# A GNN layer on one core: the set of blocks with a third quad join goes from each eighth to each fourth, from block 30 to 102

## The chip, the cores and the metric

One core of one Trainium2 chip. The time is the device time of one execution in microseconds (us). Engines are named as the profile names them: PE (matrix products; PEld its weight loads), DVE and ACT (vector and scalar engine), POOL (which issues the indirect DMAs here), SP (which issues plain DMAs).

## The reference

```python
x = -0.0005121 + 1.001 * jax.random.normal(..., (6250, 64), jnp.float32)
src = jnp.concatenate([_s, _d, _loop]); dst = jnp.concatenate([_d, _s, _loop])
_o = jnp.argsort(dst, stable=True)              # 206250 edges, ordered by dst
row, col = src, dst
msg = jnp.concatenate([x[col], edge_attr], axis=1)      # 64 + 64 columns
h = relu(msg @ W1a.T + b1a)                              # 128 columns
h = h @ W1b.T + b1b
sums = segment_sum(h, row, 6250); counts = segment_sum(ones, row, 6250)
agg = sums / maximum(counts, 1.0)[:, None]
z = relu(concatenate([x, agg], axis=1) @ W2a.T + b2a)
z = z @ W2b.T + b2b
out = layernorm(x + concatenate([z, x], axis=1) @ Wr.T + br)
```

Edges come ordered by dst, and the sum is over src, in no order. So each edge's hidden row (128 columns) has to be brought to its src.

## The kernel before

**Blocks and tiles.** The edges are padded to 124 blocks of 13 tiles of 128 edges. `fast_path` runs one loop over k = 0 to 123; loop k computes the hidden rows of block k on PE (`hidden`, line 1385) and ACT evicts them with relu into the buffer `orow` (line 1389). `orow` has four places (`ROWS = 4`): block k uses the place of block k-4. Line 1376, in `low_bits`, is ACT's first write into it in loop k, so it waits until the scatters of block k-4 have read the place.

**Scatter and sum.** A slot in DRAM is worked out for each edge, bin by bin of src (`bins_of`, `counts_of`, `slots`: lines 1059 to 1117 and 1174 to 1221, on DVE and PE). POOL then writes the rows to their slots by indirect DMA, one instruction for one tile of 128 rows (`ones_`, line 1436). Later SP reads full tiles of slots back (`read`, into `rt`), DVE makes a one-hot matrix from the node number that each row carries (`nodes_of`, line 1550), PE multiplies it with the rows (line 1570, "sums"), and the result is added to the bin's total (line 1641). Without joins there would be 124 x 13 scatters of line 1436.

**Joins.** From block 4 to 109 some tiles are joined: three tiles that go together are sorted by PE into quads, rows of four slots, and one scatter of quads (`fours`, line 1408) takes the place of three scatters of line 1436. `joined(k)` is the number of joins in block k:

```python
JOIN_FROM, JOIN_TO = 4, 110
THRICE = (*range(9, 27, 2), *range(34, 99, 8))
def joined(k):
    if not JOIN_FROM <= k < JOIN_TO:
        return 0
    return 3 if k in THRICE else 2
```

`direct(k)` = 13 - 3 x `joined(k)` tiles stay single. A block without joins has 13 scatters, one with two joins 2 + 7 = 9, one with three 3 + 4 = 7. A join costs: compare matrices `marks` (line 1253 on DVE, 1258 and 1259 on ACT), `side` and `rest` columns (lines 1267 to 1274), six products of 512 columns (line 1288) evicted to `rj` (line 1292), eight products that give the rows in quad order one loop later (line 1300, evicted at 1303), and quad ranks (lines 1117 to 1152, 1164 to 1185). Where the join count changes from one block to the next, `starts_at` (lines 924 and 927) refills a small constant on DVE.

**Order of the work.** The order on PE, ACT, DVE and SP is that of the program text in the loop body: in loop k `marks(k, 0)` and counts of block k+1; the first hidden tiles; `join_rows(k-1)`; the first half of a sum; ranks of block k+1; the last hidden tiles; `join(k, i)`; `join_places(k+1)`; the rest of the sum; the scatters of block k-2. On POOL a scheduler interleaves the last scatters of a block with the first of the next. A "pace" (from line 1416) makes the last single scatters of block k wait for a step of PE in loop k+1: with three joins those of columns 10, 11 and 12, with two those of 6, 8, 10 and 12.

**When sums are made.** A planner decides ahead which tiles are read and summed in which loop. Tiles become full by bounds that depend on how many tiles went to single slots and how many to quads, so the stages' due blocks depend on `joined`. Then it hands out groups by a rate:

```python
RATES = {0: 55, 2: 18, 3: 10}
credit += min(RATES[joined(k)], max(tiles_in(queue) - credit, 0) / (until - k))
while queue and credit > 0:
    groups_at[k].append(queue.pop(0))
    credit -= tiles_in(groups_at[k][-1:])
credit = min(credit, 0)
```

What is left, and what only the last blocks fill, is summed behind loop 123 (the sums of a loop show as line 1570, two instructions a tile). Then come the node layers, group by group of bins.

Of the kernel before, what the change touches and what calls it, by code (L numbers as in the profile page):

```python
# [469 lines left out]
LEAD = 2  # L470
JOIN, QUAD, MARKS = 3, 4, 3
JOIN_FROM, JOIN_TO = 4, 110
THRICE = (*range(9, 27, 2), *range(34, 99, 8))
JOINS = 3 if THRICE else 2
PACED = range(PRE, 123)
SIDES, ENATS, CHUNK = 2, 2, 2
# [12 lines left out]
def fast_path(  # L489
# [64 lines left out]
# [5 lines that stand above are left out]
# [1574 lines left out]
```

## Time and profile before

| | |
|---|---|
| median of 3 runs | 1561.95 us (1561.57 to 1563.52) |
| the profiled execution | 1562.71 us, its span 1560.9 us |
| busy PE / PEld | 1435.2 / 1273.7 us (92% / 82%) |
| busy DVE / ACT | 1369.4 / 1120.6 us (88% / 72%) |
| busy POOL | 1134.2 us (73%) |
| scatters of single tiles / of quads | 922 / 230 |

A row of a group reads: line, engine, operation, tile written <- tiles read, count | busy us, mean ns of one | idle time of the engine just before them, and what ended most of it. A row in order of time reads: start us, length us, engine, line, operation, tiles, count, and in brackets the idle time before it and what ended it. The loops of the program are found on PE by the first instruction of line 1113 in each, loop k being the one that works on block k's hidden rows and block k+1's counts.

### The profile page before, as it was taken

The page shows a single profiled execution, that of the slowest core. Times are in us where ns is not written, and L with a number is a line of the kernel's source. Part 1 is how long each engine was busy: PE and PEld are TensorE (multiplying, and loading weights), DVE is VectorE, ACT ScalarE, POOL GpSimd, SP SyncE. Part 2 cuts the span into 40 slices and gives each one's busy share as a digit, 9 for nine tenths or more (in the row PEclk, how much of TensorE's full clock was granted, in tenths as well). Part 3 has the DMA queues.
Part 4 walks back from the last instruction along what each step waited for, and adds up shares of the span by engine and source line. Part 5 has one row for each costly group of instructions (what it writes and reads, how often), then busy time and mean ns, then how long its engine had stood idle before and what let it go on. Part 6 is the DMA issues. An engine that isn't in the chain of part 4 may idle for free.

```text
span 1560.9 us, 33538 instructions
## 1 busy us (share of the span) xinstructions
PE 1435.2 (92%) x10958; PEld 1273.7 (82%) x10958; DVE 1369.4 (88%) x3031; ACT 1120.6 (72%) x2336; POOL 1134.2 (73%) x1215
## 2 busy tenths in 40 slices
PE   6688898879999899899998999999999999999896
PEld 5567777758888788788887888898888899999785
DVE  7589998979999899889998999999999888876786
ACT  3279999979888788787888878887877743432036
POOL 5777777777777777777777777777777777777711
PEclk9699999989999999999999999999999999999998
DMA  8878888868887888787787777676787899998873
GB/s 208 235 233 270 266 268 263 259 223 264 264 259 231 250 260 261 206 247 236 217 251 216 223 220 250 206 246 215 218 260 241 255 340 352 325 351 265 260 231 92
DMA packets 248713, 387.83 MB, mean 248 GB/s; under 512 B 43285, under 2 KB 180311, under 8 KB 248527
## 3 DMA queue, kind: packets, MB, share of 16 engines
q1 hardware_dynamic: 167661, 220.81, 50.4%
q0 software_dynamic: 47904, 122.68, 21.8%
q10 hardware_dynamic: 32962, 42.08, 8.1%
q8 instruction: 90, 1.47, 0.4%
q14 instruction: 96, 0.79, 0.2%
HBM read 214.09 MB, written 171.32 MB: 247 GB/s over the span
## 4 chain that ended last, share of the span: by engine, by line
PE 64%; DMA 13%; DVE 8%; ACT 7%; issue 4%; POOL 2%; SPq 0%; ACTq 0%; DVEq 0%; POOLq 0%
PE h_ps L1570 24%; PE h_ps L1288 13%; PE h_ps L1385 10%; PE h_ps L1300 8%; DMA rows<-orow,rowidx 8%; POOL rows L1436 2%; DMA rt<-rows 2%; DMA rows<-orow,qidx 1%; DVE marks L1253 1%; ACT marks L1258 1%; DVE oh L1550 1%; PE cnt_ps L1113 1%; ACT orow L1303 1%; PE cnt_ps L1114 1%; ACT orow L1389 1%
## 5 line engine op out<-in xcount | busy, mean ns | idle before, releaser
L1436 POOL DMA_INDIRECT rows<-orow,rowidx x922 | 898.7, 975 | 292.1 <-issue 143.0
L1570 PE MATMUL h_ps<-rt,oh 128*128 128x129 f32 x3952 | 487.3, 277 | 35.6 <-DVE oh L1550 9.9
L1570 PEld LDWEIGHTS h_ps<-rt,oh 128*128 128x128 f32 x3952 | 469.7, 193 | 49.6 <-issue 12.8
L1550 DVE TENSOR_TENSOR oh<-ramp,rt 128x768 f32<-128x768 bf16 (+4 forms) x391 | 308.2, 825 | 37.4 <-DMA rt<-rows 36.5
L1253 DVE TENSOR_TENSOR marks<-quad_ramp,ramp 128x1024 fp32r<-128x1024 f32 x230 | 276.6, 1209 | 0.0
L1408 POOL DMA_INDIRECT rows<-orow,qidx x230 | 224.0, 974 | 71.0 <-issue 25.9
L1385 PE MATMUL h_ps<-mv,rhs 124*128 124x128 f32 x1844 | 265.6, 289 | 4.4 <-ACT orow L1389 4.4
L1389 ACT ACTIVATE orow<-h_ps 128x512 f32<-128x512 f32 (+1 forms) x266 | 143.5, 539 | 173.5 <-PE h_ps L1385 163.8
L1288 PE MATMUL h_ps<-marks,side 128*128 128x512 f32 x690 | 261.7, 408 | 0.6 <-ACT mv L1354 0.6
L1300 PE MATMUL h_ps<-mv,rj 128*128 128x130 f32 x1840 | 236.7, 281 | 11.0 <-ACT orow L1389 7.4
L1385 PEld LDWEIGHTS h_ps<-mv,rhs 124*128 124x128 f32 x1844 | 233.2, 198 | 6.0 <-ACT orow L1389 4.6
L1288 PE MATMUL h_ps<-marks,rest 128*64 128x512 f32 x690 | 235.3, 395 | 0.0
L1300 PEld LDWEIGHTS h_ps<-mv,rj 128*128 128x128 f32 x1840 | 220.7, 193 | 16.9 <-ACT orow L1389 10.1
L1292 ACT COPY rj<-h_ps 128x512 f32<-128x512 f32 x230 | 131.5, 588 | 92.9 <-PE h_ps L1288 92.4
L1288 PEld LDWEIGHTS h_ps<-marks,side 128*128 128x128 f32 x690 | 131.0, 190 | 50.9 <-issue 2.1
L1259 ACT ACTIVATE marks<-marks,ones 128x512 fp32r<-128x512 f32 x230 | 166.1, 722 | 7.5
L1258 ACT ACTIVATE marks<-quad_ramp,z_act 128x512 fp32r<-128x512 f32 x230 | 166.0, 722 | 0.3 <-DVE z_act L1164 0.3
L1303 ACT ACTIVATE orow<-h_ps 128x260 f32<-128x260 f32 x460 | 151.4, 388 | 8.7 <-PE h_ps L1300 4.3
L1071 DVE TENSOR_TENSOR_SCAN had<-ramp,bins 128x400 bf16<-128x400 bf16 (+2 forms) x124 | 128.5, 1036 | 19.8 <-ACT bins L1092 6.4
L1338 ACT ACTIVATE rhs<-rhs,from_win 60x896 f32<-60x896 bf16 (+2 forms) x116 | 123.8, 1067 | 2.9
L1340 ACT ACTIVATE rhs<-rhs,ones 60x896 f32<-60x896 f32 (+2 forms) x116 | 123.5, 1065 | 2.9
L1288 PEld LDWEIGHTS h_ps<-marks,rest 128*64 128x64 f32 x690 | 93.7, 136 | 38.1 <-issue 0.6
(195 smaller groups left out, 1603.4 us busy)
## 6 DMA issues: line engine op xcount, KB each, us to landing
rt<-rows SPq DMA_DIRECT2D x194, 390.0 KB
rt<-rows SPq DMA_DIRECT2D x97, 325.0 KB
rows<-padrow ACTq DMA_DIRECT2D x24, 1040.0 KB
rhs<-in_edgeT SPq DMA_DIRECT2D x88, 224.0 KB
enat<-in_edgeJ SPq DMA_DIRECT2D x88, 192.0 KB
rows<-orow,rowidx POOLq DMA_INDIRECT x922
rt<-rows SPq DMA_DIRECT2D x40, 260.0 KB
rt<-rows SPq DMA_DIRECT2D x48, 195.0 KB
```

What stands on the lines that cost most here:

```text
L1253: nc.vector.tensor_tensor(m[:, :n, :], all_q[:, None, :].to_broadcast([P, n, QUAD * P]), z[:, :n, None].to_broadcast([P, n, QUAD * P]), op ...
L1258: nc.scalar.activation(m[:, t, :], all_q, AF.Square, bias=z_acts[k][:, i * JOIN + t : i * JOIN + t + 1], scale=-1.0)
L1259: nc.scalar.activation(m[:, t, :], m[:, t, :], AF.Relu, bias=ones[:, :1], scale=-1.0)
L1288: done[k, f"turn{i}"] = nc.tensor.matmul(ps[: w.shape[1], :], w, m[:, t, :], start=t + p == 0, stop=last and p == 1).ins.name
L1300: done[k, f"join{i}"] = nc.tensor.matmul(ps[:, j, :], rj[:, (g0 + j) * P : (g0 + j + 1) * P], m, start=True, stop=True).ins.name
L1303: nc.scalar.activation(mrow[:, g0 : g0 + 2, :], ps, AF.Relu)
L1385: done[k, c] = nc.tensor.matmul(ps[:, j, :], rhs[:WIDE, of * P : (of + 1) * P], m[:WIDE, :H], start=True, stop=True).ins.name
L1389: nc.scalar.activation(orow_of(k, k0, n)[:, :, :H], ps[:, :n, :], AF.Relu)
L1408: s = nc.gpsimd.indirect_dma_start(out=qep.rows.rearrange("(q r) f -> q (r f)", r=QUAD), out_offset=bass.IndirectOffsetOnAxis(ap=qidx[:, q ...
L1436: s = nc.gpsimd.indirect_dma_start(out=ep_.rows, out_offset=bass.IndirectOffsetOnAxis(ap=rowidx[:, k % RING * BLK + j : k % RING * BLK + j ...
L1550: nc.vector.tensor_tensor(res[:, at_tile : at_tile + nb * n, :], ramp[:, None, :].to_broadcast([P, nb * n, P]), node[:, :, None].to_broadc ...
L1570: m = nc.tensor.matmul(of_bin(b), oh[:, at, :], rows, start=i == 0, stop=i == len(of) - 1)
```

## The change

`THRICE` holds ten more blocks: 30, 38, 46, 54, 62, 70, 78, 86, 94 and 102; 34, 42 and so on to 98 stay, and 9 to 25 too.

```diff
-THRICE = (*range(9, 27, 2), *range(34, 99, 8))
+THRICE = (*range(9, 27, 2), *range(30, 103, 4))
```

In each of the ten, three tiles that had single scatters form a third join. All else follows from `joined(k)`: NJOIN goes from 230 to 240, the scatters of line 1436 from 922 to 892, those of line 1408 from 230 to 240. The edge loads of such a block change shape (64 x 896 to 64 x 512 and 128 x 384 to 128 x 576), not number. `starts_at` is called 20 times more. The planner's input changes with it: stages that were due at blocks 54, 78 and 102 are due at 55, 81 and 107, those of quads at 47, 68, 81 and 94 instead of 49, 70, 84 and 98, and tiles of sums move between loops. In loops 31 to 109 there are 1026 tiles before and 962 after, in 110 to 120 564 and 568, in loop 121 40 and 60, and 40 more behind loop 121. By tiles in a loop, the loops 31 to 109 are: before, 5 with none, 55 with 12, six with 18, two with 20, eight with 24, three others; after, 5 with none, 63 with 12, two with 18, six with 24, three others.

On POOL around block 30 (its rows are read from orow_142; orow_141 is block 29's, orow_143 block 31's; qidx marks a scatter of quads). Before:

```order
L1408 DMA rows_64<-orow_141,qidx 84320x520 x2
L1436 DMA rows_64<-orow_141,rowidx 337280x130
L1436 DMA rows_64<-orow_142,rowidx 337280x130 x2
L1436 DMA rows_64<-orow_141,rowidx 337280x130
L1436 DMA rows_64<-orow_142,rowidx 337280x130
L1436 DMA rows_64<-orow_143,rowidx 337280x130 x2
L1408 DMA rows_64<-orow_142,qidx 84320x520 x2
L1436 DMA rows_64<-orow_142,rowidx 337280x130 x2
```

The same place after:

```order
L1408 DMA rows_64<-orow_141,qidx 85600x520 x2
L1436 DMA rows_64<-orow_141,rowidx 342400x130 x3
L1436 DMA rows_64<-orow_142,rowidx 342400x130 x2
L1436 DMA rows_64<-orow_143,rowidx 342400x130 x2
L1408 DMA rows_64<-orow_142,qidx 85600x520 x3
L1436 DMA rows_64<-orow_142,rowidx 342400x130 x2
L1436 DMA rows_64<-orow_143,rowidx 342400x130 x2
```

Block 30 has seven single scatters and two of quads before, four and three after; its neighbours keep theirs, in a slightly different interleaving.

On PE at the end of loop 30 (marks_155 to 157 are the three compare matrices in rotation, side_158 and rest_160 the columns of block 30), one piece of the difference:

```order
 L1288 MATMUL h_ps<-marks_157,rest_160 64x512 x2
 L1288 MATMUL h_ps<-marks_157,side_158 128x512
+L1288 MATMUL h_ps<-marks_155,side_158 128x512
+L1288 MATMUL h_ps<-marks_155,rest_160 64x512
+L1288 MATMUL h_ps<-marks_155,side_158 128x512
+L1288 MATMUL h_ps<-marks_155,rest_160 64x512 x2
+L1288 MATMUL h_ps<-marks_155,side_158 128x512
```

Six products of 512 columns are added, the third join of block 30; the other nine new blocks get the same.

On PE behind the last hidden tiles (rhs_151 is block 123's, rt and oh a read tile and its one-hot matrix), where only sums are left before the first node group (line 1976):

```order
 L1570 MATMUL h_ps<-rt,oh 128x129 x10
 L1385 MATMUL h_ps<-mv,rhs_151 128x128 x3
-L1570 MATMUL h_ps<-rt,oh 128x129 x241
+L1570 MATMUL h_ps<-rt,oh 128x129 x281
 L1976 MATMUL h_ps<-ident,agg 128x128 x3
 L1570 MATMUL h_ps<-rt,oh 128x129 x3
```

Forty tiles of sums moved from the loops to this place.

## The prediction

> **What bounds the kernel now.** I read the page first, then POOL's own rows in order of time, then the start of each loop on PE, then the waits, and last the end of the program. The page's head and the two groups of scatters:
>
> ```profile
> span 1560.9 us, 33538 instructions
> ...
> PE 1435.2 (92%) x10958; PEld 1273.7 (82%) x10958; DVE 1369.4 (88%) x3031; ACT 1120.6 (72%) x2336; POOL 1134.2 (73%) x1215
> ...
> L1436 POOL DMA_INDIRECT rows<-orow,rowidx x922 | 898.7, 975 | 292.1 <-issue 143.0
> ...
> L1408 POOL DMA_INDIRECT rows<-orow,qidx x230 | 224.0, 974 | 71.0 <-issue 25.9
> ```
>
> By busy share PE leads and POOL looks a quarter idle. But POOL's 1152 scatters have idle time of 292.1 + 71.0 = 363.1 us in front of them, 0.32 each, and its rows show that this is no waiting. Two neighbours, and three rows far from them (start, length, idle before):
>
> ```profile
> 406.68 0.97 POOL L1436 DMA_INDIRECT rows<-orow,rowidx  x1 [0.30 <-PE cnt_ps L1117]
> ...
> 1034.45 0.96 POOL L1436 DMA_INDIRECT rows<-orow,rowidx  x1 [0.30 <-issue]
> 1035.72 0.97 POOL L1436 DMA_INDIRECT rows<-orow,rowidx  x1 [0.30 <-ACT rj L1292]
> ...
> 1456.42 0.96 POOL L1436 DMA_INDIRECT rows<-orow,rowidx  x1 [0.30 <-issue]
> ...
> 1489.46 0.97 POOL L1436 DMA_INDIRECT rows<-orow,rowidx  x1 [0.30 <-issue]
> ```
>
> The gap is 0.30 whatever is named as its releaser, and 1035.72 - 1034.45 = 1.27: one scatter each 1.27 us. The stage from 676.6 to 1259.3 confirms it (columns: length, then busy time and count for PE, PE's loads, DVE, ACT, POOL; then clock, DMA share, GB/s):
>
> ```profile
> 676.60:1259.30 582.70, 563.88 (x4381) 501.39 (x4382) 548.77 (x1198) 475.64 (x935) 443.68 (x457) 1.00 0.77 236
> ```
>
> 457 x 1.27 = 580 of 582.7 us: POOL is issuing without a pause. PE (563.88, 97%) and DVE (548.77, 94%) are nearly as full. Three engines are within a few per cent of each other, so a change that takes from one and gives to two must be summed for each.
>
> How PE is held by POOL: line 1376 writes into the buffer of rows that the scatters of block k-4 have read. ACT waits there, its next eviction is late, and PE stands. The totals of the waits from 342 to 1458 us (us, times, longest), ACT's and PE's:
>
> ```profile
> ACT orow L1376 <- DMA rows<-orow,rowidx: 22.9, 14, 3.2
> ...
> PE h_ps L1570 <- ACT orow L1389: 8.8, 5, 3.6
> PE h_ps L1570 <- ACT orow L1303: 7.3, 3, 4.2
> ...
> PE h_ps L1300 <- ACT orow L1389: 2.6, 3, 1.3
> ```
>
> A single case is loop 46, from 511.44 to 527.64; PE's rows, and ACT's row in it:
>
> ```profile
> 492.31 0.33 PE L1113 MATMUL cnt_ps<-had,less_ones 128*128 128x400 bf16 x1
> 503.36 0.33 PE L1113 MATMUL cnt_ps<-had,less_ones 128*128 128x400 bf16 x1
> 511.44 0.33 PE L1113 MATMUL cnt_ps<-had,less_ones 128*128 128x400 bf16 x1 [0.45 <-DVE ways L1174]
> 518.47 2.95 PE L1570 MATMUL h_ps<-rt,oh 128*128 128x129 f32 x12 [3.64 <-ACT orow L1389]
> 527.64 0.33 PE L1113 MATMUL cnt_ps<-had,less_ones 128*128 128x400 bf16 x1
> ```
>
> ```profile
> 517.72 0.20 ACT L1376 CAST orow<-lo 128x7 f32<-128x7 bf16 x1 [2.95 <-DMA rows<-orow,rowidx]
> ```
>
> Loop 46 took 527.64 - 511.44 = 16.20 us, where loop 44 with the same work took 503.36 - 492.31 = 11.05: a wait of 2.95 on ACT cost 5.15. So 22.9 is a floor of what POOL costs PE this way.
>
> The end of the sums:
>
> ```profile
> 1423.66 9.10 PE L1570 MATMUL h_ps<-rt,oh 128*128 128x129 f32 x80
> ...
> 1437.73 19.67 PE L1570 MATMUL h_ps<-rt,oh 128*128 128x129 f32 x146
> 1464.13 12.55 PE L1570 MATMUL h_ps<-rt,oh 128*128 128x129 f32 x98 [6.73 <-DVE oh L1550]
> ```
>
> PE has summed all it may by 1457.40, then waits 6.73 us for the first rows that need POOL's block 121 (POOL was at 1457.7 then). From 1464.13 on the rest is sums and the node layers, untouched by the change.
>
> **The change part by part.** Sums are made against the profiled execution: 1562.71 us, span 1560.9, so 0.76 above the median of 1561.95.
>
> *POOL.* Ten blocks lose three L1436 scatters each and gain one L1408: 30 - 10 = 20 fewer, 20 x 1.27 = 25.4 us. The order shows no scatter added elsewhere. Rows of block 121 would so be ready at about 1464.13 - 25.4 = 1438.7, if POOL still never waits.
>
> *PE and DVE, the joins.* Around the triple block 90 of before, the loops begin on PE and on DVE at:
>
> ```profile
> 994.98 0.27 PE L1113 MATMUL cnt_ps<-had,less_ones 128*128 128x250 bf16 x1
> 1005.23 0.33 PE L1113 MATMUL cnt_ps<-had,less_ones 128*128 128x400 bf16 x1
> 1016.32 0.33 PE L1113 MATMUL cnt_ps<-had,less_ones 128*128 128x400 bf16 x1
> 1027.36 0.33 PE L1113 MATMUL cnt_ps<-had,less_ones 128*128 128x400 bf16 x1
> 1037.53 0.33 PE L1113 MATMUL cnt_ps<-had,less_ones 128*128 128x400 bf16 x1
> 1050.66 0.33 PE L1113 MATMUL cnt_ps<-had,less_ones 128*128 128x400 bf16 x1
> ```
>
> ```profile
> 995.29 1.21 DVE L1253 TENSOR_TENSOR marks<-quad_ramp,ramp 128x1024 fp32r<-128x1024 f32 x1
> ...
> 1007.03 1.21 DVE L1253 TENSOR_TENSOR marks<-quad_ramp,ramp 128x1024 fp32r<-128x1024 f32 x1
> ...
> 1018.21 1.21 DVE L1253 TENSOR_TENSOR marks<-quad_ramp,ramp 128x1024 fp32r<-128x1024 f32 x1
> ...
> 1028.26 1.21 DVE L1253 TENSOR_TENSOR marks<-quad_ramp,ramp 128x1024 fp32r<-128x1024 f32 x1
> ...
> 1038.31 1.21 DVE L1253 TENSOR_TENSOR marks<-quad_ramp,ramp 128x1024 fp32r<-128x1024 f32 x1
> ```
>
> On PE loops 89 to 92 take 10.25, 11.09, 11.04 and 10.17; the last is plain, the first three hold the third join: 32.38 - 3 x 10.17 = 1.87 us. This price contains everything the join brings (marks, side, turned rows, ranks, three direct tiles less). On DVE the first two take 11.74 and 11.18 against 10.05: 22.92 - 20.10 = 2.82. Ten joins cost 18.7 by PE and 28.2 by DVE. DVE has gaps elsewhere in the stage (6%), PE fewer (3%), so I take a value nearer PE's: **+22**, bounds 18.7 and 28.2. ACT's two marks per join are off the path: it is busy 475.64 of 582.7.
>
> *The sums that move.* By the order, loops 31 to 109 hold 1026 tiles of sums before and 962 after; the 64 come later: 4 in loops 110 to 120, 20 in loop 121, 40 behind it. Late they cost 9.10 / 40 = 0.2275 each (the x80 row; two instructions a tile): 14.6 us. What they free is not even. Six loops of 18 tiles, two of 20 and eight of 24 become two, none and six; 12-tile loops rise from 55 to 63. An 18-tile loop against a 12-tile one:
>
> ```profile
> 1150.91 0.33 PE L1113 MATMUL cnt_ps<-had,less_ones 128*128 128x400 bf16 x1
> 1163.13 0.33 PE L1113 MATMUL cnt_ps<-had,less_ones 128*128 128x400 bf16 x1
> ```
>
> 12.22 - 10.17 = 2.05, or 0.34 a tile; the 24-tile loop 93 took 1050.66 - 1037.53 = 13.13, 0.25 a tile more. At 0.25 to 0.29 for the mix the 64 free 16 to 18.6 us; I take 17.1, so **-2.5**. Bounds: 0.34 gives -7.2; loop 45, empty, took 8.08, hence (10.17 - 8.08) / 12 = 0.17 a tile, and +3.7.
>
> *The waits for the ring.* Each added join takes 2 x 1.27 = 2.54 us from POOL and puts about 2 on PE, so PE's lead over POOL shrinks by some 4.5 us at each. Four lie before loop 50: 18 us of a lead at which ACT in loop 46 was late by only 2.95. The waits should go: **-24**, a little over the 22.9 measured on ACT because of loop 46's 5.15 for 2.95. Bounds: -12, if empty loops followed by 24-tile ones (there still are five and six) bring half of them back; -27.
>
> *The last wait.* PE's arrival at the last sums moves by 22 - 2.5 - 24 = -4.5, to 1457.40 - 4.5 = 1452.9; rows are ready at 1438.7. The wait of 6.73 goes whole, **-6.7**. What is late next is PE and DVE themselves, 14 us behind POOL. Nothing comes back as long as POOL loses under 14 us to waits of its own, which it now may: its last scatters of a block wait for PE's next loop (the pace, line 1416), and behind such a scatter all later ones stand.
>
> *Rest.* Twenty more calls of starts_at put small memsets on DVE around each triple; they are inside the 2.82. Edge loads change shape, not number; DMA share was 0.77.
>
> **Sum:** 22 - 2.5 - 24 - 6.7 = -11.2; 1562.71 - 11.2 = 1551.5 us. On the median's basis it would be 0.8 lower; I leave it.
>
> **The rivals.**
>
> *Nearly all of POOL's 25.4 comes through.* For it: POOL is the one engine with no pause. Then 1562.71 - 25.4 = 1537.3 is the limit, 1537 to 1543 the case. It needs joins at 18.7, sums at -7.2 and waits at -27: -15.5 - 6.7 = -22.2, 1540.5. Against it: PE at 97% of its stage.
>
> *Nothing net.* Joins at 24.4, waits recovered only 16, sums -1.7: 24.4 - 1.7 - 16 - 6.7 = 0, so 1562.7. For it: PE and POOL become so close that each wait of one for the other is paid in full.
>
> *Slower, by DVE.* The mark compare and the memsets of a third join lie on DVE in full, and DVE sits in front of PE in each loop through the ranks (line 1174). At 28.2 for the joins, 0 for the sums and 15 for the waits: 28.2 - 15 - 6.7 = +6.5, **1569**. It decides from the point where the joins cost over 6.7 us more than the waits and moved sums give back. For it: 94% busy, 10.05 us a plain loop back to back. Against it: that interval is also PE's 10.17, so part of DVE's excess is PE's.
>
> *POOL was never the bound.* By busy share POOL at 73% has time to spare, 20 scatters less free nothing, no ring wait goes, and PE and DVE pay 22 - 2.5: 1562.71 + 19.5 = **1582**. Against it stand the 0.30 in every gap and the 22.9 us that ACT waited for scatters. The Trainium skill, "Perfetto Trace Analysis", section "Identifying the Most-Contended Engine", calls the most-contended engine the one with the highest occupancy, to be worked on first, with the caution that TensorE be judged by its weight loads and not by matmul time. By that rule this change works on the wrong engine: POOL's 73% is under the loads' 82% and DVE's 88%. The trace bears the rule out only if the 0.30 between scatters counts as free, and 457 x 1.27 = 580 of 582.7 says that it isn't.
>
> That the change does not take place is excluded by the order: 18 triple blocks become 28.
>
> **How the numbers follow.** 0.2%, 3.1 us, is about what a measurement here can tell from no change. Forecast as summed, gains of 5 to 18: 0.60. All of POOL's share: 0.12. Nothing net: 0.12. Slower by DVE: 0.12. POOL not the bound: 0.04. Faster 0.72, same 0.12, slower 0.16. The range runs from the best of the bounds, 18.7 - 7.2 - 27 - 6.7 = -22.2 (1541), to 1567, a third of the way into the slower case, which I spread from 1565 to 1573; left out are two thirds of it, the 0.04, and half of the best case, 0.18 together.
>
> **What would show it.** Right: POOL's last scatter near 1464 to 1475 instead of 1489.46; under 8 us of ACT waiting in line 1376; no wait of PE for line 1550 before the last sums; POOL gaps over 0.30 in front of L1436 that name PE. Each four loops with one triple should take some 42.5 on PE, as loops 89 to 92 do now. Wrong: the 6.73 still there with POOL's rows late (then POOL stayed the bound or was starved), L1376 waits over 15 us, or loops with a third join over 2.8 us dearer than plain ones.

## The result, and the profile after

| | before | changed |
|---|---|---|
| median | 1562.24 us, 21 runs (1559.76 to 1565.48) | 1568.20 us, 21 runs (1562.50 to 1571.61) |
| ratio | | 1.0036, 95% interval 1.0028 to 1.0044 |

The change makes the kernel slower by 0.36%, some 5.6 us. The forecast was 1551.5 (1541 to 1567) with 0.72 on faster; the rival "slower, by DVE" had 1569 and a chance of 0.12.

The first profile of the changed kernel fell on an execution of 1562.62 us, at the low end of its runs. A second one, of 1567.4, is near the median and is read here (again_b, the same kernel); the first is used to see how far one execution differs from another. The page of again_b:

```profile
span 1565.5 us, 33825 instructions
...
PE 1446.0 (92%) x11058; PEld 1279.0 (82%) x11058; DVE 1393.4 (89%) x3093; ACT 1136.0 (73%) x2376; POOL 1114.9 (71%) x1195
...
L1436 POOL DMA_INDIRECT rows<-orow,rowidx x892 | 868.8, 974 | 295.0 <-issue 136.6
...
L1408 POOL DMA_INDIRECT rows<-orow,qidx x240 | 234.5, 977 | 74.5 <-issue 22.6
```

POOL has its 20 scatters less, and its last one starts 13 us earlier than the 1489.46 of before:

```profile
1476.61 0.96 POOL L1436 DMA_INDIRECT rows<-orow,rowidx  x1 [0.30 <-issue]
```

The two waits that the forecast wanted gone are gone. ACT's waits from 342 to 1458 us, in full, hold no row of line 1376 any more: ACT no longer stands in front of the ring, the four places of `orow` (before: 22.9 us). And PE goes into the last sums with 0.42 us of wait instead of 6.73:

```profile
ACT orow L1389 <- PE h_ps L1385: 153.2, 52, 11.6
ACT rj L1292 <- PE h_ps L1288: 79.2, 121, 0.9
ACT orow L1303 <- PE h_ps L1300: 13.8, 6, 5.4
ACT rj L1292 <- issue: 0.2, 1, 0.2
ACT marks L1258 <- DVE z_act L1164: 0.2, 1, 0.2
```

```profile
1443.52 28.60 PE L1570 MATMUL h_ps<-rt,oh 128*128 128x129 f32 x226
1472.55 11.18 PE L1570 MATMUL h_ps<-rt,oh 128*128 128x129 f32 x98 [0.42 <-PE h_ps L1570]
```

Yet PE comes to this place only at 1472.1, having done 40 tiles of sums more on the way, where before it came at 1457.4 and stood until 1464.1. To see where the time is, both profiles are divided at the same loops: the stretches begin at loops 31, 58, 85 and 110, and the last ends where loop 122 begins. Columns: stretch, its length, then busy time and count for PE, PE's loads, DVE, ACT, POOL; clock, DMA share, GB/s. Before:

```profile
352.50:644.80 292.30, 285.95 (x2179) 251.70 (x2178) 268.77 (x596) 251.16 (x520) 222.78 (x229) 0.99 0.84 253
644.80:951.70 306.90, 290.01 (x2211) 255.00 (x2211) 281.64 (x625) 252.57 (x505) 233.72 (x241) 0.99 0.76 227
951.70:1236.80 285.10, 278.73 (x2175) 248.12 (x2173) 273.85 (x592) 233.67 (x458) 217.13 (x224) 1.00 0.77 237
1236.80:1417.90 181.10, 179.36 (x1586) 176.88 (x1584) 147.48 (x259) 71.84 (x98) 137.80 (x143) 1.00 1.02 333
```

Changed (again_b):

```profile
347.80:642.80 295.00, 292.05 (x2210) 256.35 (x2210) 276.23 (x616) 257.14 (x534) 224.25 (x233) 0.99 0.82 254
642.80:935.30 292.50, 283.45 (x2153) 246.16 (x2151) 278.00 (x628) 255.40 (x516) 222.66 (x230) 1.00 0.74 229
935.30:1234.80 299.50, 285.06 (x2170) 251.77 (x2170) 278.79 (x601) 238.28 (x469) 216.57 (x222) 0.99 0.70 219
1234.80:1423.70 188.90, 185.54 (x1634) 182.60 (x1633) 154.80 (x270) 72.64 (x101) 143.56 (x149) 1.00 1.03 332
```

The second stretch, where most of the waits for the ring stood, is 14.4 us shorter. The third is 14.4 longer and takes all of it back; the last is 7.8 longer, with 24 tiles of sums more. The time ahead of loop 31 was 4.7 us shorter in this execution and the part from loop 122 on 1.2: -4.7 + 2.7 - 14.4 + 14.4 + 7.8 - 1.2 = +4.6, the difference of the spans. Some 3 of the third stretch's 14.4 us belong to the execution and not to the change: in the first profile of the same kernel it took 296.1 us, at a granted clock of 1.00 instead of 0.99:

```profile
935.60:1231.70 296.10, 281.76 (x2170) 248.76 (x2170) 278.44 (x601) 238.34 (x469) 218.31 (x224) 1.00 0.72 222
```

*PE.* What PE waits for has changed its name, and hardly its size. In loops 31 to 109, before, the two largest rows that name DVE (the prediction shows the rows that name ACT's `orow`):

```profile
PE cnt_ps L1113 <- DVE ways L1174: 4.0, 8, 2.0
PE h_ps L1570 <- DVE oh L1550: 1.8, 1, 1.8
```

The same loops in again_b, with the two rows that still name ACT's `orow`:

```profile
PE cnt_ps L1113 <- DVE ways L1174: 8.8, 13, 2.3
PE h_ps L1570 <- DVE oh L1550: 5.1, 3, 2.1
...
PE h_ps L1300 <- ACT orow L1389: 2.7, 3, 1.2
PE h_ps L1570 <- ACT orow L1389: 1.9, 4, 0.6
```

All rows of PE together come to 30.7 us before and 27.3 after. Those that name ACT's `orow` fall from 18.7 to 4.6, those that name DVE rise from 6.0 to 15.1, the others from 6.0 to 7.6. What PE does outside its waits rises from 853.6 to 859.7.

*POOL.* Before, no scatter from loop 31 on starts more than 0.32 us after the one in front of it has ended: POOL never waits. In again_b 17 scatters do, all in loops 91 to 109, by 15.5 us over the 0.30 of each. Two neighbours:

```profile
1013.33 0.96 POOL L1436 DMA_INDIRECT rows<-orow,rowidx  x1 [3.30 <-PE h_ps L1570]
1015.39 0.96 POOL L1436 DMA_INDIRECT rows<-orow,rowidx  x1 [1.10 <-ACT orow L1303]
```

POOL has caught up with PE there and stands until PE's rows are ready. (In the first profile it is 15 scatters and 9.8 us.)

*DVE.* All its waits in the same loops of again_b:

```profile
DVE rest L1274 <- ACT side L1267: 12.1, 14, 2.1
DVE of_quads L1127 <- PE cnt_ps L1117: 3.3, 3, 1.4
DVE part L1641 <- PE h_ps L1570: 2.0, 2, 1.4
```

DVE waits for 17.4 of the 887.0 us of these loops: its own work and its own small gaps take 869.6. Before, it waited for 28.1 of 884.3 (three rows, and 2.1 in four small ones), which leaves 856.2:

```profile
DVE rest L1274 <- ACT side L1267: 20.6, 22, 2.4
DVE of_quads L1127 <- PE cnt_ps L1117: 3.8, 5, 1.6
DVE part L1641 <- PE h_ps L1570: 1.6, 1, 1.6
```

In loops 68 to 83 of again_b DVE waits for 0.2 of 175 us, PE for 6.6: there DVE sets the pace. In the third stretch they wait for each other in turn, in loops with 24 tiles of sums above all. One of them as an example, 85: it takes 17.78 us (935.30 to 953.08; 16.2 in the first profile, since the granted clock was 0.90 in this loop and 1.00 in that). PE's rows, then DVE's:

```profile
945.22 1.50 PE L1570 MATMUL h_ps<-rt,oh 128*128 128x129 f32 x12
948.54 4.70 PE L1570 MATMUL h_ps<-rt,oh 128*128 128x129 f32 x24 [1.83 <-DVE oh L1550]
```

```profile
947.40 0.23 DVE L1185 TENSOR_SCALAR qidx<-s_q,part_f 128x3 int32<-128x3 f32 x1
947.54 3.54 DVE L1550 TENSOR_TENSOR oh<-ramp,rt 128x768 f32<-128x768 bf16 x4
951.00 0.41 DVE L1641 TENSOR_TENSOR part<-part,h_ps 128x258 f32<-128x258 f32 x1
951.33 1.22 DVE L1253 TENSOR_TENSOR marks<-quad_ramp,ramp 128x1024 fp32r<-128x1024 f32 x1
```

The one-hot matrices come in one piece behind the quad ranks of the next, triple, block. DVE has no gap in these rows, and PE waits for it.

### The profile page after: what moved, and what is told of

Its sections match the earlier page's. It is cut to its first block, busy times and chain, and to the rows that moved or that the text cites. A ratio compares the mean times of both kernels' runs of the same rounds, so it can differ in the third digit from the quotient of the medians.

```text
span 1560.8 us, 33825 instructions
## 1 busy us (share of the span) xinstructions
PE 1452.5 (93%) x11058; PEld 1284.3 (82%) x11058; DVE 1392.5 (89%) x3093; ACT 1136.0 (73%) x2376; POOL 1117.0 (72%) x1195
## 4 chain that ended last, share of the span: by engine, by line
PE 53%; DVE 18%; ACT 10%; DMA 10%; issue 6%; POOL 2%; ACTq 0%; SPq 0%; DVEq 0%; POOLq 0%
PE h_ps L1570 22%; PE h_ps L1288 9%; DMA rows<-orow,rowidx 8%; PE h_ps L1385 8%; PE h_ps L1300 6%; DVE marks L1253 3%; DVE oh L1550 2%; ACT marks L1258 2%; POOL rows L1436 1%; ACT rhs L1340 1%; ACT rj L1292 1%; ACT marks L1259 1%; ACT orow L1303 1%; DVE rest L1274 1%; DVE row L1212 1%
## 5 line engine op out<-in xcount | busy, mean ns | idle before, releaser
L1436 POOL DMA_INDIRECT rows<-orow,rowidx x892 | 870.6, 976 | 289.4 <-issue 139.7
L1550 DVE TENSOR_TENSOR oh<-ramp,rt 128x768 f32<-128x768 bf16 (+4 forms) x391 | 307.9, 823 | 29.0 <-DMA rt<-rows 28.1
L1408 POOL DMA_INDIRECT rows<-orow,qidx x240 | 234.8, 978 | 75.2 <-issue 21.0
L1253 DVE TENSOR_TENSOR marks<-quad_ramp,ramp 128x1024 fp32r<-128x1024 f32 x240 | 287.5, 1207 | 0.0
L1288 PE MATMUL h_ps<-marks,side 128*128 128x512 f32 x720 | 272.0, 408 | 0.7 <-ACT mv L1354 0.6
L1389 ACT ACTIVATE orow<-h_ps 128x384 f32<-128x384 f32 (+1 forms) x256 | 138.6, 541 | 176.2 <-PE h_ps L1385 168.5
L1385 PE MATMUL h_ps<-mv,rhs 124*128 124x128 f32 x1784 | 255.9, 288 | 2.9 <-ACT orow L1389 2.9
L1300 PE MATMUL h_ps<-mv,rj 128*128 128x130 f32 x1920 | 245.7, 281 | 8.4 <-ACT orow L1389 6.6
L1288 PE MATMUL h_ps<-marks,rest 128*64 128x512 f32 x720 | 245.1, 394 | 0.0
L1300 PEld LDWEIGHTS h_ps<-mv,rj 128*128 128x128 f32 x1920 | 230.3, 194 | 13.0 <-ACT orow L1389 8.6
L1385 PEld LDWEIGHTS h_ps<-mv,rhs 124*128 124x128 f32 x1784 | 225.2, 198 | 4.6 <-ACT orow L1389 3.2
L1303 ACT ACTIVATE orow<-h_ps 128x260 f32<-128x260 f32 x480 | 159.1, 388 | 19.5 <-PE h_ps L1300 13.4
```

The source lines that it names most:

```text
L1253: nc.vector.tensor_tensor(m[:, :n, :], all_q[:, None, :].to_broadcast([P, n, QUAD * P]), z[:, :n, None].to_broadcast([P, n, QUAD * P]), op ...
L1288: done[k, f"turn{i}"] = nc.tensor.matmul(ps[: w.shape[1], :], w, m[:, t, :], start=t + p == 0, stop=last and p == 1).ins.name
L1300: done[k, f"join{i}"] = nc.tensor.matmul(ps[:, j, :], rj[:, (g0 + j) * P : (g0 + j + 1) * P], m, start=True, stop=True).ins.name
L1303: nc.scalar.activation(mrow[:, g0 : g0 + 2, :], ps, AF.Relu)
L1385: done[k, c] = nc.tensor.matmul(ps[:, j, :], rhs[:WIDE, of * P : (of + 1) * P], m[:WIDE, :H], start=True, stop=True).ins.name
L1408: s = nc.gpsimd.indirect_dma_start(out=qep.rows.rearrange("(q r) f -> q (r f)", r=QUAD), out_offset=bass.IndirectOffsetOnAxis(ap=qidx[:, q ...
```

## The experiments

Theory 1: DVE has become the bound, and a third join costs its time. Theory 2: the planner's later and clumped sums cost it. Theory 3: a few early joins end the waits for the ring, and the later ones only cost. The runs came on two kinds of chip. On one, the kernel before takes 1560 us as at first; on the other some 1945 or 1963. There PE has 179.8 us of "issue", waits for nothing that the profile shows (4.5 in again_b), and the mean granted clock is 0.92 (0.98 in again_b). Which of these makes that chip slow, and what the "issue" waits are for, is not shown; an instruction transfer falls into only 15 of PE's 162 such waits in the first of these runs (again). Only the first kind of chip is used for the argument. Ratios to the kernel before on the same chip, with 95% intervals:

| run | chip like the first | the other chip |
|---|---|---|
| changed kernel | 1.0046 (1.0032 to 1.0059) | 0.9985 (0.9958 to 1.0013) |
| plan alone | 1.0018 (1.0008 to 1.0029) | 1.0001 (0.9968 to 1.0035) |
| changed, constant kept | 0.9999 (0.9988 to 1.0010) | 0.9898 (0.9862 to 0.9934) |
| five early triples | 0.9925 (0.9912 to 0.9939) | 0.9929 (0.9894 to 0.9965) |
| four late triples | 1.0038 (1.0023 to 1.0054) | 0.9997 (0.9964 to 1.0029) |
| five early, late plan | 0.9964 (0.9950 to 0.9978) | 0.9987 (0.9956 to 1.0017) |
| five early, constant kept | 1.0022 (1.0011 to 1.0033) | 0.9902 (0.9869 to 0.9935) |
| changed, third join on ACT | | 0.9970 (0.9939 to 1.0000), 0.9964 (0.9940 to 0.9989) |
| three early triples | | 1.0018 (0.9994 to 1.0043) |
| five early, third join on ACT | | 0.9983 (0.9955 to 1.0010) |

**The changed kernel again.**

> The changed kernel once more, for a second profile beside the first, whose execution was among the fastest of its kernel. All theories: 1565 to 1571 us by the median. Theory 1 (DVE has become the bound: a third join costs it 2.8 us, and waits of PE for DVE have taken the place of the waits for the ring): DVE back to back in loops 60 to 110, PE's losses there named with lines 1550, 1174 or 1113. Theory 2 (the plan of the sums: tiles come later and in clumps of 24): the loops that take longer than in the first profile are those of 24 tiles and the stretch behind loop 121.

> [...] All theories, if this chip is like the first: 1.003 to 1.0045 of before, some 1567 us; Theory 1 (DVE has become the bound in loops 60 to 110) wants PE's losses there at lines 1550, 1174 and 1113.

The first of the two came on the other chip (1938.89 us, 0.9985) and can say nothing here. On the first kind of chip the changed kernel takes 1567.4 us, like the 1568.20 of the result. PE's losses name the lines that Theory 1 named, 1113 and 1550. Theory 2 wanted the second profile to be longer than the first in the loops of 24 tiles and behind loop 121. It is longer in loops 31, 85 and 108, of 0, 24 and 18 tiles, by 1.3 to 1.7 us each, and in these three the granted clock was 0.83 to 0.91, in the first profile 1.00. So the two profiles differ by the clock, and decide nothing between the theories.

**The plan alone.** The joins of before, the stages' loops of the changed kernel:

```diff
+        open_at = [{57: 58, 81: 84, 105: 110}.get(at, at) for at in open_at]
         opens = sorted({*open_at, NGR})
```

> The kernel before with its own joins, but three stages of sums opened where the changed kernel opens them (loops 58, 84 and 110 instead of 57, 81 and 105): 968 tiles in loops 31 to 109 instead of 1026, as late and as clumped as after. Theory 2 (the plan costs the time): 1566 to 1571, like the changed kernel. Theory 1 (DVE and its joins): 1560 to 1564, like before, since no join is added.

> The kernel before with three stages of sums opened as late as in the changed one, no join added. Theory 2: 1.002 to 1.005 of before, 1565 to 1570 us. Theory 1: 0.998 to 1.001.

1562.87 us, 1.0018: between the two. ACT's waits in line 1376 rise to 31.3 us. The last wait of PE is gone here too (0.42), with no scatter less: 40 more tiles lie in front of it.

**Which joins.** Five early ones:

```diff
-THRICE = (*range(9, 27, 2), *range(34, 99, 8))
+THRICE = (*range(9, 27, 2), *range(30, 63, 4), *range(66, 99, 8))
```

> Only four of the ten added triples: 30, 38, 46 and 54; from 62 on as before. Theory 1 with a share for each join: four tenths of the loss, 1563 to 1566. Theory 3 (four joins before block 58 already end the waits for the ring, which the first profile shows at no later loop, and the six later ones only cost DVE and PE): 1548 to 1557. Theory 2: 1563 to 1567, its sums are clumped as in the changed kernel (seven loops of 24 tiles).

> Only the added triples 30, 38, 46 and 54. Theory 3 (four early joins end the waits for the ring, six later ones only cost): 0.991 to 0.998 of before, 1548 to 1559 us. A share for each join (Theory 1 alone): 1.001 to 1.002. Theory 2 (clumped sums): 1.001 to 1.003.

The runs named early_four hold five added triples: 30, 38, 46, 54 and 62; the "four" of their names and expectations is wrong. 1549.39 us, 0.9925: half of the change gains 11.6 us. No row of line 1376 stands among ACT's waits, and the last wait is 0.43. The second and third stretch:

```profile
648.60:940.10 291.50, 284.83 (x2182) 249.03 (x2181) 278.85 (x625) 255.16 (x513) 222.32 (x228) 1.00 0.77 232
940.10:1231.00 290.90, 281.83 (x2202) 251.04 (x2200) 276.80 (x594) 232.60 (x453) 221.61 (x228) 1.00 0.76 236
```

The second stretch has the whole gain of the ten (15.4 shorter than before). The third gives back 5.8 instead of 14.4, though no join is added in it, and the part from loop 122 on is 9.9 shorter. POOL has no gap over 0.32 us from loop 31 on, and its last scatter comes 13.6 us earlier than before, about the ten scatters of 1.27 that were taken from it:

```profile
1475.89 0.97 POOL L1436 DMA_INDIRECT rows<-orow,rowidx  x1 [0.30 <-issue]
```

From here to the end it is 71.5 us, as from 1489.46 before. So with five triples POOL is still the bound, and all that is taken from it comes through. The ten take ten scatters more from it, and its last one comes at 1476.61, no earlier: there POOL waits for PE, and the end follows PE's sums, 88.9 us behind.

Four late ones, at 78, 86, 94 and 102, with as many tiles of sums in loops 31 to 109 (1016), in 110 to 121 and behind them as with the five early:

```diff
-THRICE = (*range(9, 27, 2), *range(34, 99, 8))
+THRICE = (*range(9, 27, 2), *range(34, 75, 8), 78, 82, 86, 90, 94, 98, 102)
```

> Four triples added late (78, 86, 94, 102) instead of early; the sums' tiles by stage are the same as with the four early ones (1016, 564, 50). Theory 3 (what counts is that the join comes before the waits for the ring in loops 46 to 82): those waits stay, 1.000 to 1.004 of before. If only the number of joins counts: 0.992 to 0.994.

> Four triples added at 78, 86, 94 and 102 instead of early, the same tiles of sums by stage. Theory 3 (the place counts: before the waits for the ring): 0.999 to 1.004 of before, with ACT's waits in line 1376 still some 20 us. Number alone: 0.992 to 0.994.

1.0038: slower than before. Line 1376 still waits, 11.9 us in all, not the 20 that I expected. The stretches show that the place counts, whatever the fifth join is worth: the second stretch keeps its length (306.3 us), and the third, which holds three of the four, is 12.0 longer than before:

```profile
954.00:1251.10 297.10, 283.47 (x2184) 250.17 (x2182) 280.12 (x605) 238.83 (x470) 218.11 (x225) 1.00 0.73 226
```

POOL stands 14 times in loops 97 to 111, for 12.4 us, and its last scatter starts at 1492.74, 3.3 us later than before with eight scatters less. Late joins take from POOL what it then spends waiting for PE.

Three early ones, 30, 38 and 46:

```diff
-THRICE = (*range(9, 27, 2), *range(34, 99, 8))
+THRICE = (*range(9, 27, 2), *range(30, 51, 4), *range(58, 99, 8))
```

> Three added triples, 30, 38 and 46. The runs named early_four held five (30, 38, 46, 54 and 62). Theory 3 with DVE's price: if three already end the waits for the ring, two joins' 2.8 us each are saved, 0.989 to 0.992 of before; if they do not (each takes 4.5 us of lead, and 14 are to be taken), 0.992 to 0.997, and ACT waits 5 to 15 us in line 1376.

This came on the other chip only, where 1.0018 (0.9994 to 1.0043) is no gain. It fits none of the two answers that I had given it; that three are too few is not shown for the first kind of chip.

**The plan under the early joins.** The five early triples, with two stages of sums opened later:

```diff
+        open_at = [{83: 84, 107: 110}.get(at, at) for at in open_at]
         opens = sorted({*open_at, NGR})
```

> The four early triples, but two stages of sums opened as late as in the changed kernel (84 and 110 instead of 83 and 107). Theory 2 in its narrower form (the six later joins cost through the plan, which lets the stage of loop 107 open only at 110, behind the last join): 0.998 to 1.004 of before. Theory 1 (they cost through their own work on DVE): 0.992 to 0.995.

> The four early triples with the two stages opened as late as in the changed kernel, on a chip like the first. Of the some 18 us by which six later triples cost more than the four early ones gain, this is the plan's part. Theory 2: 0.997 to 1.003 of before, 1556 to 1566 us. Theory 1 (the later joins' own work): 0.992 to 0.995, 1549 to 1553 us.

0.9964, between the theories: the late plan costs the five 0.0039, some 6 us. The later five joins make up the rest to 1.0046: 0.0082, 12.8 us, 2.6 us each. ACT waits 23.1 us in line 1376 here, in a kernel faster than the one before, so that total does not by itself measure a loss; 17.6 of it stand behind loop 109. The second and third stretch, for the comparison with again_b, which has nearly the same tiles in each:

```profile
646.60:933.50 286.90, 279.20 (x2134) 243.61 (x2132) 272.92 (x616) 250.83 (x507) 218.65 (x224) 1.00 0.77 229
933.50:1219.60 286.10, 276.67 (x2154) 245.76 (x2154) 272.18 (x585) 233.99 (x457) 218.02 (x224) 1.00 0.75 228
```

Two of the five later joins lie in the second stretch: 292.5 - 286.9 = 5.6, 2.8 each. Three lie in the third: 299.5 - 286.1 = 13.4, 4.5 each; with the first profile of the changed kernel, at a clock of 1.00, it is 296.1 - 286.1 = 10.0, 3.3 each. (This profile is of 1548.91 us, 5 below its median, so these are upper values.) A direct case is loops 77 to 80, all of 12 tiles, where block 78 has two joins with the five and three with the ten: 40.6 us and 44.8 us, 4.2 more. DVE does not wait in either; it is busy for 39.2 and 42.9 us.

**DVE's work made less.** The constant of the scan in a tile for each count of joins, instead of a refill at each change (... stands for lines left out):

```diff
-        words = steady[:, RAMP + 2 : RAMP + 2 + HALF * T]
-        on = words.bitcast(BF16)
+        ons = {}
...
+            words = (
+                const.tile([P, HALF * t + HALF * t % 2], F32, name=f"starts{joints}") if joints
+                else steady[:, RAMP + 2 : RAMP + 2 + HALF * T]
+            )
+            ons[joints] = words.bitcast(BF16)
...
-            if joined(k) != joined(k - 1):
-                starts_at(joined(k))
...
-            nc.vector.tensor_tensor_scan(had, on[:, : 2 * HALF * t], oh, 0.0, op0=ALU.mult, op1=ALU.add)
+            nc.vector.tensor_tensor_scan(had, ons[joined(k)][:, : 2 * HALF * t], oh, 0.0, op0=ALU.mult, op1=ALU.add)
```

> The changed kernel, with the small constant for the scan kept in three tiles, one for each count of joins, instead of refilled at each change of the count (lines 924 to 929, some 0.6 us of DVE, twice for each lone triple block; 56 refills go). Theory 1 (DVE is the bound): 1545 to 1558, since 10 to 25 of these 35 us of DVE come through. Theory 2 (the plan): 1565 to 1570, no change from the changed kernel.

> The scan's constant in three tiles instead of 56 refills on DVE, on the changed kernel. Theory 1 (DVE is the bound): 0.988 to 0.998 of before, 1544 to 1559 us, since 10 to 25 of the 35 us of refills come through. Theory 2 (the plan of the sums): 1.002 to 1.0045, no change from the changed kernel.

The edit does two things. It takes the refills from DVE, and it moves the constant for two and three joins: `steady` is a tile in PSUM (its pool has `space=PSUM`), the tiles of `const` lie in SBUF. The last section shows what that does to POOL.

0.9999, 7.4 us under the changed kernel: less than Theory 1 wanted (0.988 to 0.998), and not what Theory 2 wanted (1.002 to 1.0045). In its profile (of 1555.01 us, 5 below its median) DVE's time outside its waits in loops 31 to 109 falls by 28 us, to 841.4, and the loops by 8, to 878.8; DVE's waits rise to 37.4. So DVE's time counts, but most of what is taken from it does not come through: POOL has no gap over 0.32 us again, with scatters that have become longer. On the other chip the same edit gained 0.0087.

> The four early triples together with the scan's constant in three tiles. Theory 1 with 3 (with the ring's waits gone the loops run at DVE's pace): the refills' share comes on top, 0.986 to 0.990 of before, 1539 to 1546 us. If POOL is what holds the four-triple kernel: 0.992, no better than without.

> The four early triples and the scan's constant in three tiles. If the loops run at DVE's pace once the ring's waits are gone: 0.984 to 0.990 of before, 1537 to 1545 us; if POOL holds the four-triple kernel: 0.991 to 0.993, and ACT's waits in line 1376 come back.

A miss in the number, against every theory on the first kind of chip: 1.0022 where the five triples alone give 0.9925, while on the other chip it is among the two best. What the second expectation said for POOL as the bound did come: ACT waits again in line 1376, and the last wait is back, larger than ever:

```profile
ACT orow L1379 <- DMA rows<-orow,rowidx: 35.0, 19, 6.6
```

```profile
1464.93 18.09 PE L1573 MATMUL h_ps<-rt,oh 128*128 128x129 f32 x134 [9.05 <-DVE oh L1553]
```

(Three lines more stand ahead of it in this kernel: 1379 is 1376, and so on.) So POOL is late against PE, with as many scatters as in early_four_b. Its scatters themselves take longer; the group in early_four_b, then here:

```profile
L1436 POOL DMA_INDIRECT rows<-orow,rowidx x907 | 885.8, 977 | 286.0 <-issue 141.4
```

```profile
L1439 POOL DMA_INDIRECT rows<-orow,rowidx x907 | 899.9, 992 | 285.9 <-issue 134.2
```

14.1 us more for the same 907. POOL never waits from loop 31 on, and its last scatter starts at 1490.76, 14.9 us later than with the five triples alone. That is the kernel's loss: the five-triple kernel is bound by POOL, and its scatters have become longer. The last section shows by what.

**The third join's compare moved to ACT.** On the changed kernel, and in early_five_act on the five early triples:

```diff
-            n = JOIN - ON_ACT
+            n = JOIN - (2 if i == 2 else ON_ACT)
```

> The changed kernel, with the third join's second compare on ACT too (two ACT instructions of 0.72 us instead of some 0.55 us of DVE, in 28 blocks). Theory 1 (DVE's pace): 0.994 to 1.001 of before, 5 to 12 us better than the changed kernel. Theory 2: 1.003 to 1.006; worse than that if ACT, at 82% in the middle, becomes late.

> All ten triples, with the third join's second compare on ACT (0.55 us of DVE less, two ACT instructions of 0.72 us more, in 28 blocks, 19 of them from 30 on: 10 us of DVE there). Theory 1 (the later joins cost DVE's time): 0.998 to 1.002 of before, 4 to 10 us better than the changed kernel. Theory 2 (the plan alone): 1.003 to 1.006. Above 1.006: ACT was no slack.

> The five early triples, with the third join's second compare on ACT. If DVE still sets the pace with five: 0.988 to 0.991 of before. If POOL and DVE are even there: 0.992 to 0.994. If the freed DVE lets PE run ahead into the ring again, as in early_four_starts_b: 0.995 to 1.002, and line 1376 waits over 15 us.

All three came on the other chip. On the changed kernel 0.9970 and 0.9964 against 0.9985 without: the right way for Theory 1, but the intervals overlap. On the five, 0.9983 against 0.9929: no gain. For the first kind of chip they decide nothing.

## Why the prediction was wrong

By its own steps:

- **POOL's 25.4 us.** Right in size: 20 scatters of 1.27. But POOL's last scatter came 13 us earlier, not 14 to 25. POOL waits 15.5 us in loops 91 to 109, mostly in rows that name PE and ACT. The text had such waits among its signs of being right, and held that up to 14 us of them would cost nothing.
- **The last wait, -6.7.** Right: 0.42 instead of 6.73. But it proves nothing of POOL: the late plan alone, with no join added, ends this wait too.
- **The waits for the ring, -24.** This is the step that failed. The forecast took 24 us off PE's time because ACT would no longer wait in line 1376. ACT no longer does, but PE's waits in loops 31 to 109 fell by 3.4 us, from 30.7 to 27.3. The rows of PE that name ACT's `orow` had 18.7 us to give, not 24, and gave 14.1; in their place waits for DVE came, 9.1 us more, and 1.6 of others. The sum took PE's stalls as free time. The text named what would be late next, "PE and DVE themselves, 14 us behind POOL", and did not ask how soon. Loops 31 to 109 were to take 884.3 + 22 - 17.1 - 24 = 865.2 and took 887.0: 21.8 more, of which 20.6 are these waits and 1.2 is PE's time outside them, which rose by 6.1 where 22 - 17.1 = 4.9 was forecast.
- **The joins, +22.** Too low for the later ones. The choice of 2.2 lay "nearer PE's" 1.87; where DVE does not wait, its 2.82 was the row to take. The later five cost 2.6 each beside the plan (0.0082 of 1561 us, from intervals that leave some 2.0 to 3.2), and block 78's costs 4.2 in loops 77 to 80, so that the sign "loops with a third join over 2.8 us dearer than plain ones" came there.
- **The moved sums, -2.5.** Wrong in sign as far as runs show it: opening the stages late costs 0.0018 on the joins of before, although it also ends the last wait of 6.73 there, and 0.0039 on the five early ones: some 3 and 6 us.

A check on DVE would have warned of the sum. DVE's time outside its waits was 856.2 before; ten joins at 2.82 add 28.2. For loops of 865.2 us the 64 tiles that leave them would have had to free 19.2 us of DVE; by the row of line 1550 above (3.54 us for 24 tiles) their one-hot matrices free some 9.4, an estimate. DVE in fact took 869.6 outside its waits. That floor alone explains only 4.4 of the 21.8 us: the other 17.4 are DVE's own waits for ACT and PE.

The rival "slower, by DVE" had joins at 28.2, sums at 0, waits at 15 and so 1569; 1568.2 came. Its number came close; that its parts did is not shown. The rule of the Trainium skill, "Perfetto Trace Analysis", section "Identifying the Most-Contended Engine", that the engine with the highest occupancy is the one to work on first, is not borne out here: POOL at 73% was the bound, and with ten scatters fewer the five triples reach 0.9925. But after those ten PE with DVE was late, and the next ten gained nothing.

What stays open: how the third stretch's loss divides between DVE's price, the clumps of 24 tiles and ACT, each waiting for the others in turn. That DVE's time counts is shown in loops 68 to 83, where it does not wait, and by the run without refills, which was faster although its scatters were longer; how much it would have gained with the constant left in PSUM was not tried. The runs that moved a compare to ACT came on a chip that could not tell.

The version that beats both is the five early triples: 1549.39 us, 0.9925 (0.9912 to 0.9939) of before.

## What to carry to other kernels

When several engines are within a few per cent of each other, take each one's time for the stage with its waits removed (length less what it waited for), and add what the change gives to it. No stage can become shorter than the longest of these sums, and it can stay well above it, since the engines also wait for each other in turn. A wait that goes is worth its time only until the next engine is late. So a trade of one engine's time for another's pays only where the relieved engine is behind: once it shows gaps of its own, further units only cost. Try half of the change, and each half's place. And an edit that takes work from one engine may also move a tile to another memory; look at every engine's mean time for one instruction before putting the result down to the work.

## What the runs showed of the hardware

A scatter on POOL is not always 0.97 us. In early_four_starts_b (five early triples, constant in SBUF) one beside its neighbour:

```profile
1179.47 0.97 POOL L1439 DMA_INDIRECT rows<-orow,rowidx  x1 [0.30 <-DMA rows<-orow,rowidx]
1180.74 1.69 POOL L1439 DMA_INDIRECT rows<-orow,rowidx  x1 [0.30 <-issue]
```

DVE in the same time:

```profile
1180.66 0.99 DVE L1074 TENSOR_TENSOR_SCAN had<-starts,bins 128x400 bf16<-128x400 bf16 x1
1181.57 0.51 DVE L1273 TENSOR_TENSOR side<-ramp,rel_j 128x360 fp32r<-128x360 bf16 x1
1182.21 0.56 DVE L1277 TENSOR_TENSOR rest<-enat,side 128x384 fp32r<-128x384 f32 x1
```

The scatter starts 0.08 us into DVE's scan and lasts 0.72 longer than its neighbour. This is no single case. In that run 64 scatters start during a scan whose constant is one of the new tiles in SBUF (`starts`): 44 of them last over 1.1 us, and the mean is 1.23. The later in the scan such a scatter starts, the less it is lengthened (0.45 us at 0.34 into it, 0.20 at 0.60), as if it were held until the scan is nearly over; those that start in its first 0.04 us are not lengthened. In the same run 25 scatters start during a scan whose constant is still in PSUM, and none is longer than 0.97. In early_four_b, where every scan takes its constant from PSUM, 95 scatters start during a scan, and none lasts over 0.99. So it is not that scatters fall together with scans more often; it is where the scan's constant lies. 64 scatters at 0.26 more make 17 us, enough for POOL's 14.9.

The Trainium skill, "SBUF — State Buffer", section "Who interferes with whom", says that a DVE instruction with two inputs in SBUF contends with a GpSimd instruction that reads SBUF. These rows agree with that: the scan's other input, `bins`, lies in SBUF in all of these kernels. Line 1274, whose two inputs `enat` and `side` both lie in SBUF, fits too: in early_four_b 17 of the 41 scatters that start during it last over 1.1 us. Other ways in which the two memories differ for DVE were not tried. On the other chip the scatters are lengthened as well (31 of 55 in early_four_starts), and the kernel gains all the same; what bounds it there was not looked into.
